# A window-attention and Fourier kernel: the order of ScalarE, VectorE and GpSimd written by hand as well as TensorE's, with attention times values ahead of the scores and the softmax in three parts

## The chip, the cores and the metric

One core of a Trainium2 chip. The metric is the device time of one execution in microseconds; the median of some runs is quoted. In the lines of the profile PE is TensorE's matmuls, PEld its weight loads, DVE is VectorE, ACT ScalarE, POOL GpSimd and SP SyncE; L12 is line 12 of that kernel, `out<-in` names what an instruction writes and reads, and brackets hold the engine's idle time before it and what ended it.

## The reference, cut to what matters

Two pre-normed residual layers on an image batch of 32 x 56 x 56 x 128, all fp32:

```python
x = x + swin_attention(group_norm(x))     # shifted 7x7 windows, 4 heads, rel. bias + mask, softmax, projection
x = x + fourier_block(group_norm(x))      # DCT along w and h, 32 modes mixed, inverse DCT, then
                                          # relu(h @ W1 + b1) @ W2 + b2, hidden width 512
```

## The kernel before

The kernel walks over 256 "rows": one row is the eight windows of one band of seven image lines, eight rows make an image. In each row, attention of one image runs next to a slice of the Fourier layer of the image before it. Row r computes q, k, v and the scores; two rows later the softmax is transposed, multiplied by the values and projected. The slices of the Fourier layer differ: I number the rows of an image c0 to c7 after them. c0 to c2 transform, c3 to c5 mix the modes, c4 to c7 transform back; all but c3 hold a group of the feed-forward (320 tokens in c4, 256 in c5, 512 elsewhere). At the ends of c2, c3 and c4 groups of the next image are transposed, and c5 does its norm.

TensorE's order is that of the source; the other engines are ordered by a scheduler:

```python
with tc.manual_schedule(engines={mybir.EngineType.PE}):
    ...
    for cycle in range(...):
        full_first(cycle)      # transposes of row-2, q, k of this row, zT transposes, feed-forward in
        ...
        half_columns(cycle)    # v of this row; DCT or mode mixing
        quarters(cycle)        # scores of this row, inverse DCT, values of row-2
        full_last(cycle, norm) # norm, feed-forward out, projection of row-2, groups of the next image
```

The parts that the argument touches (cut):

```python
def attn_qk(im, i):                       # ScalarE and VectorE empty k in turns
    for h in range(NH):
        if h % 2: nc.vector.tensor_scalar(dst, pk3[hs], im.bias[hs, 1:2], None, ALU.add)
        else:     nc.scalar.activation(dst, pk3[hs], AF.Identity, bias=im.bias[hs, 1:2])

def attn_scores(im, i, r):
    ...                                   # 64 matmuls
    for hp in range(2): nc.vector.tensor_tensor(a3, ps[hp], bm, ALU.add)
    nc.vector.tensor_reduce(mx2, a3, axis=AX.X, op=ALU.max)
    nc.gpsimd.tensor_tensor(a3, a3, mx2..., ALU.subtract)
    nc.scalar.activation(a3, a3, AF.Exp)
    nc.vector.tensor_reduce(sm2, a3, axis=AX.X, op=ALU.add)
    nc.vector.reciprocal(rs2, sm2)
    nc.gpsimd.tensor_tensor(a3, a3, rs2..., ALU.mult)

def image_norm(im):                       # small operations of the next image's norm
    nc.tensor.matmul(pg, lhsT=gavg, rhs=mv[:, 0:1], ...)
    nc.vector.tensor_copy(gm, pg[:, 0:1])
    nc.vector.tensor_tensor(d, mv[:, 0:1], gm, ALU.subtract)
    nc.vector.scalar_tensor_tensor(out=e, in0=d, scalar=d, in1=mv[:, 1:2], op0=ALU.mult, op1=ALU.add)
    yield
    nc.tensor.matmul(pv, lhsT=gavg, rhs=e, ...)      # the "second norm matmul"
    ...
```

PSUM, the memory that TensorE writes, is used as two rings of four banks: pa for attention, pc for the Fourier layer. Other names in the lines: oT is attention times values, xw a transposed group of the next image, hid the hidden layer of the feed-forward, zT the transposed modes that the inverse transform starts from, xf its result. A matmul group can start only when the bank that was taken four allocations earlier has been emptied.

## Time and profile before

| | kernel before |
|---|---|
| median time, us | 4475.1 (3 runs, 4466.23 to 4480.21) |
| TensorE busy, share of the span | 91% |
| mean granted clock | 0.963 |
| TensorE idle per image, us (mean of 27 or 28 images) | 10.1 |
| time at half clock per image, us | 7.9 |

The last two rows are read from the trace: between the first q matmul of one row and of the next, idle time is what no matmul record covers, and the clock records say how long the clock was at half. An image takes 135.1 us.

### The profile page before, as it was taken

The numbers are of one execution on the slowest core, as the hardware profiler recorded it, in microseconds if no ns is written. First come the engines' busy times: TensorE is split into PE (matmuls) and PEld (weight loads), VectorE is DVE, ScalarE is ACT, GpSimd is POOL, SyncE is SP. The second block draws the span as 40 slices with busy tenths as digits, with TensorE's granted clock in tenths as the row PEclk, the third lists the DMA queues.
The fourth block names the chain that finished last, engine by engine and source line by source line (L and its number), as shares of the span: only waits on it lengthen the run. The fifth ranks groups of instructions, "written<-read, shape, count | busy, mean of one in ns | idle before, by whom it ended". The sixth has DMA issues, their size and how long they took to land.

```text
span 4472.3 us, 165690 instructions
## 1 busy us (share of the span) xinstructions
PE 4051.8 (91%) x74816; PEld 3326.9 (74%) x74816; DVE 2485.8 (56%) x5078; ACT 2258.0 (50%) x4065; POOL 1386.7 (31%) x1358
## 2 busy tenths in 40 slices
PE   4789999899999999999999999999999999999999
PEld 3667777777777777777777777777777777777777
DVE  3655565555555555555555655555555555555551
ACT  1345555455555555555555555555545555555544
POOL 2323332233323333332333332333322333333321
PEclk8789999999999999999999999999999999999999
DMA  3111222212222212222212222212222212222112
GB/s 85 47 33 53 68 69 67 63 43 61 66 68 69 59 45 63 69 69 67 61 44 64 69 69 67 56 46 68 69 67 69 55 46 68 63 72 64 46 51 66
DMA packets 533831, 273.07 MB, mean 61 GB/s; under 512 B 29796, under 2 KB 532741, under 8 KB 532869
## 3 DMA queue, kind: packets, MB, share of 16 engines
q1 hardware_dynamic: 522072, 257.04, 21.9%
q8 instruction: 587, 9.62, 0.9%
q10 hardware_dynamic: 11052, 5.44, 0.5%
q14 instruction: 120, 0.97, 0.1%
HBM read 159.60 MB, written 102.76 MB: 59 GB/s over the span
## 4 chain that ended last, share of the span: by engine, by line
PE 70%; DVE 15%; POOL 6%; ACT 3%; issue 3%; DMA 2%; ACTq 1%; SPq 0%; POOLq 0%; DVEq 0%
PE pc L645 15%; PE pc L665 9%; PE pa L340 6%; PE pa L320 6%; PE pc L560 5%; PE pa L380 5%; PE pc L523 5%; POOL a L362 4%; PE pa L304 4%; DVE a L353 4%; PE pa L299 4%; DVE mx L361 4%; PE pa L436 4%; DVE sm L366 3%; ACT a L365 3%
## 5 line engine op out<-in xcount | busy, mean ns | idle before, releaser
L665 PE MATMUL pc<-wff,hid 128*128 128x128 f32 (+1 forms) x6400 | 786.5, 280 | 44.7 <-DVE xf L613 23.7
L665 PEld LDWEIGHTS pc<-wff,hid 128*128 128x128 f32 (+1 forms) x6400 | 737.8, 191 | 69.4 <-DVE xf L613 30.4
L362 POOL TENSOR_TENSOR a<-a,mx 128x784 f32<-128x784 f32 x256 | 388.5, 1518 | 1182.8 <-DVE mx L361 1170.0
L353 DVE TENSOR_TENSOR a<-pa,bm 128x392 f32<-128x392 f32 x512 | 266.3, 562 | 859.4 <-PE pa L340 859.4
L645 PE MATMUL pc<-xf,wff 128*128 128x512 f32 (+2 forms) x1792 | 710.4, 539 | 0.0
L653 ACT ACTIVATE hid<-pc,b1sb 128x512 f32<-128x512 f32 (+2 forms) x896 | 537.2, 632 | 77.8 <-PE pc L645 70.7
L365 ACT ACTIVATE a<-a 128x784 f32<-128x784 f32 x256 | 223.6, 873 | 677.4 <-POOL a L362 677.4
L368 POOL TENSOR_TENSOR a<-a,rs 128x784 f32<-128x784 f32 x256 | 389.0, 1519 | 545.7 <-DVE rs L367 519.9
L635 POOL TENSOR_TENSOR res<-res,b2sb 128x512 f32<-128x512 f32 (+2 forms) x256 | 263.7, 1035 | 905.1 <-DMA res<-scr 739.5
L645 PEld LDWEIGHTS pc<-xf,wff 128*128 128x128 f32 x1792 | 329.9, 190 | 275.1 <-issue 228.1
L366 DVE TENSOR_REDUCE sm<-a 128x16 f32<-128x784 f32 x256 | 248.2, 970 | 474.1 <-ACT a L365 474.1
L310 DVE TENSOR_SCALAR k_bd<-pa,bqkv 32x392 f32<-32x392 f32 x512 | 320.7, 626 | 269.3 <-ACT k_bd L312 261.3
L436 PE MATMUL pa<-wproj,oT 128*112 128x128 f32 x1792 | 266.5, 292 | 195.5 <-DVE oT L425 128.4
L436 PEld LDWEIGHTS pa<-wproj,oT 128*112 128x112 f32 x1792 | 226.9, 188 | 218.8 <-issue 167.2
L455 ACT ACTIVATE sq<-xl 112x384 f32<-112x384 f32 (+1 forms) x256 | 147.8, 578 | 440.0 <-DVE xl L444 333.9
L386 DVE COPY aT<-pa 128x512 f32<-128x512 f32 x512 | 336.7, 679 | 0.7 <-PE pa L380 0.7
L380 PE MATMUL pa<-ident,a 128*128 128x128 f32 x2048 | 314.7, 302 | 13.3 <-DVE xl L444 12.4
L340 PE MATMUL pa<-k_bd,q 64*64 64x49 f32 x16384 | 310.0, 221 | 17.3 <-ACT k_bd L312 8.6
L312 ACT ACTIVATE k_bd<-pa,bqkv 32x392 f32<-32x392 f32 x512 | 298.1, 582 | 54.7 <-PE pa L304 19.5
L320 PEld LDWEIGHTS pa<-wn,xw 128*64 128x64 f32 x4096 | 219.5, 137 | 133.9 <-issue 60.3
L252 POOL TENSOR_TENSOR xl<-xl,bproj 112x384 f32<-112x384 f32 (+1 forms) x256 | 285.0, 1141 | 80.9 <-PE pa L237 77.7
L340 PEld LDWEIGHTS pa<-k_bd,q 64*64 64x64 f32 x16384 | 273.0, 135 | 46.3 <-issue 15.8
(86 smaller groups left out, 6260.9 us busy)
## 6 DMA issues: line engine op xcount, KB each, us to landing
htok<-scr SPq DMA_DIRECT2D x256, 196.0 KB
res<-scr SPq DMA_DIRECT2D x160, 256.0 KB
out_dram<-res SPq DMA_DIRECT2D x128, 256.0 KB
scr<-xl SPq DMA_DIRECT2D x128, 224.0 KB
xl<-in_x_dram SPq DMA_DIRECT2D x32, 784.0 KB
xl<-in_x_dram SPq DMA_DIRECT2D x32, 672.0 KB
scr<-xl SPq DMA_DIRECT2D x128, 168.0 KB
out_dram<-res SPq DMA_DIRECT2D x96, 128.0 KB
```

Source lines behind the costliest of these rows:

```text
L320: nc.tensor.matmul(pv[w % 2 * JP : (w % 2 + 1) * JP, (w // 2) * C : (w // 2 + 1) * C], lhsT=im.xw[i][:, w * WT : w * WT + JP], rhs=im.w[:, ...
L340: nc.tensor.matmul(ps[hp][u * JP : (u + 1) * JP, w * WT : (w + 1) * WT], lhsT=q[cs, w * WT : w * WT + JP], rhs=k_bd[cs, w, u], start=True, ...
L353: nc.vector.tensor_tensor(a3, ps[hp][:, :RT].rearrange("p (m j) -> p m j", j=WT), bm[:, i // (NWR - 1), hp], ALU.add,)
L362: nc.gpsimd.tensor_tensor(a3, a3, mx2.unsqueeze(2).to_broadcast([P, 2 * NR, WT]), ALU.subtract)
L365: nc.scalar.activation(a3, a3, AF.Exp)
L366: nc.vector.tensor_reduce(sm2, a3, axis=AX.X, op=ALU.add)
L368: nc.gpsimd.tensor_tensor(a3, a3, rs2.unsqueeze(2).to_broadcast([P, 2 * NR, WT]), ALU.mult)
L380: nc.tensor.transpose(pt[:, m * P : (m + 1) * P], a[:, hp, 2 * pr : 2 * pr + 2].rearrange("p w j -> p (w j)"), ident,)
L436: nc.tensor.matmul(pp[:TC, (n - n0) * C : (n - n0 + 1) * C], lhsT=oT[:, (n - base) * TC : (n - base + 1) * TC], rhs=wproj, start=True, sto ...
L645: nc.tensor.matmul(ph[:, :n], lhsT=wff1[:, f * P : (f + 1) * P], rhs=xff[:, t0 : t0 + n], start=True, stop=True,)
L653: nc.scalar.activation(hf[:, :n], ph[:, :n], AF.Relu, bias=b1sb[:, f : f + 1])
L665: nc.tensor.matmul(pf[:m, c * C : (c + 1) * C], lhsT=im.hid[f][:, c * P : c * P + m], rhs=wff2[:, f], start=(f == 0), stop=(f == NF - 1),)
```

## The change

Its intent: take the remaining waits off TensorE by deciding the order on every engine. Values go before the scores, so that their result (oT) can be emptied while the scores run. The softmax becomes add, maximum and subtract after the scores, exp at the end of the row, sum and multiply in the next row. The norm and the statistics are cut into smaller steps. Groups of the next image go ahead of the projection.

```diff
-        nc.vector.reciprocal(rs2, sm2)
+    def attn_exp(r):
+        nc.scalar.activation(a3, a3, AF.Exp)
+    def attn_divide(r):
+        nc.vector.tensor_reduce(sm, a3, axis=AX.X, op=ALU.add)
+        nc.vector.reciprocal(rs, sm)
+        nc.gpsimd.tensor_tensor(a3, a3, rs..., ALU.mult)
 ... full_first
             for width, g in back_groups(c):
                 modes_transpose(im, width, g)
+        if row(cycle - 1)[0]:
+            attn_divide(cycle - 1)
+        next(norm)
         ...                                    # feed-forward in, statistics
+        next(norm)
 ... quarters, now small_tiles
+        attn_values(im, i, cycle - 2)
         attn_scores(im, i, cycle)
         ...                                    # modes_back
-        attn_values(im, i, cycle - 2)
 ... full_last
         ff_out(...)
+        attn_exp(cycle)
+        next(norm)
+        ...image_group(images[b + 1], j)
         attn_project(im, j)
-        ...image_group(images[b + 1], j)
-    with tc.manual_schedule(engines={mybir.EngineType.PE}):
+    with tc.manual_schedule(engines={ET.PE, ET.Activation, ET.DVE, ET.Pool}):
```

(The norm and the statistics gain `yield`s at other places, and the norm starts one row earlier.)

## The prediction

> **What bounds the kernel now.** I read the page first (busy time by engine, chain by engine), then cut the trace into windows, one for each row of attention, then TensorE's waits, and last the timeline of the rows with the longest waits.
>
> ```profile
> PE 4051.8 (91%) x74816; PEld 3326.9 (74%) x74816; DVE 2485.8 (56%) x5078; ACT 2258.0 (50%) x4065; POOL 1386.7 (31%) x1358
> ...
> PE 70%; DVE 15%; POOL 6%; ACT 3%; issue 3%; DMA 2%; ACTq 1%; SPq 0%; POOLq 0%; DVEq 0%
> ```
>
> TensorE is 91% busy and 70% of the chain; no other engine is near full. TensorE's program stays nearly the same, so the change can only win or lose the idle part, and the time at a lowered clock that idling brings. Eight rows make one image. Here is one image, a window per row (columns: length; busy us and instructions of PE, PEld, DVE, ACT, POOL; granted clock; DMA share; GB/s). I call the rows c0 to c7 in this order.
>
> ```profile
> 2212.25:2229.49 17.24, 17.03 (x320) 13.92 (x319) 9.81 (x22) 9.88 (x16) 3.65 (x5) 1.00 0.71 184
> 2229.49:2244.44 14.95, 14.95 (x263) 11.72 (x261) 8.04 (x17) 7.89 (x13) 4.12 (x5) 1.00 0.43 105
> 2244.44:2261.08 16.64, 15.85 (x269) 12.32 (x268) 9.96 (x20) 9.22 (x17) 5.69 (x6) 1.00 0.15 42
> 2261.08:2274.78 13.70, 11.68 (x306) 9.97 (x305) 8.09 (x17) 7.29 (x15) 6.66 (x8) 1.00 0.15 43
> 2274.78:2292.84 18.06, 16.80 (x343) 14.68 (x343) 11.24 (x24) 11.53 (x23) 7.28 (x8) 1.00 0.11 30
> 2292.84:2312.46 19.62, 16.79 (x319) 15.10 (x317) 10.81 (x28) 9.87 (x21) 6.94 (x7) 0.88 0.17 47
> 2312.46:2330.24 17.78, 16.63 (x275) 12.68 (x275) 9.32 (x19) 7.10 (x13) 4.42 (x4) 0.94 0.03 9
> 2330.24:2346.23 15.99, 15.23 (x261) 11.86 (x260) 9.95 (x21) 7.37 (x13) 4.41 (x4) 1.00 0.16 43
> ```
>
> Length minus PE busy is TensorE's idle time: 2.0 us in c3, 1.3 in c4, 2.8 in c5, under 1.2 elsewhere. Averaged over the 27 images between rows 30 and 250 the idle is 0.84, 0.45, 0.71, 2.09, 1.24, 3.11, 0.83, 0.79 us: 10.1 of 135.1 us. In c5 and c6 the clock falls too: 7.9 us per image run at half clock (averaged the same way), which costs up to 3.9. Both together, 14 us or 10%, are all that a better order could win. What TensorE waits for:
>
> ```profile
> PE pa L436 <- DVE oT L425: 128.4, 96, 4.3
> PE pa L436 <- DVE ve L274: 65.2, 31, 3.6
> ...
> PE pc L665 <- DVE xf L613: 23.7, 42, 0.8
> ```
>
> The output projection (L436) waits for the evacuation of attention times values (oT). Row c3 shows why:
>
> ```profile
> 2267.33 1.15 PE L340 MATMUL pa<-k_bd,q 64*64 64x49 f32 x64
> ...
> 2268.51 1.04 DVE L353 TENSOR_TENSOR a<-pa,bm 128x392 f32<-128x392 f32 x2 [2.87 <-PE pa L340]
> ...
> 2269.59 0.97 DVE L361 TENSOR_REDUCE mx<-a 128x16 f32<-128x784 f32 x1
> ...
> 2270.47 0.66 DVE L425 TENSOR_SCALAR oT<-pa,bqkv 128x147 f32<-128x147 f32 x3
> 2270.70 1.52 POOL L362 TENSOR_TENSOR a<-a,mx 128x784 f32<-128x784 f32 x1 [5.31 <-DVE mx L361]
> 2271.28 1.10 PE L436 MATMUL pa<-wproj,oT 128*112 128x128 f32 x8 [1.64 <-DVE oT L425]
> ...
> 2272.25 0.87 ACT L365 ACTIVATE a<-a 128x784 f32<-128x784 f32 x1 [2.07 <-POOL a L362]
> ...
> 2273.03 1.24 ACT L247 COPY xw<-pa 128x392 f32<-128x392 f32 x3
> ...
> 2273.63 1.06 PE L380 MATMUL pa<-ident,a 128*128 128x128 f32 x8
> ```
>
> Scores (L340) end at 2268.4; VectorE adds the mask and takes the maximum before it empties oT, so TensorE stands for 1.64 us. The last two lines matter later: exp, then the copies of the next image's groups (L247), end 5.8 us after the scores.
>
> **What the Trainium skill says.** "TensorE: Matmul & The Clock Gate", Part 1, table of states: half clock after an idle window of about 3.4 us, full clock after a busy one. The trace agrees on the two levels and on the free-running window, but less idleness is enough: of the 61 falls to half clock the median came after a window in which PE was 40% busy, and none above 68%; a gap of about 2 us does it. The same page, section "Architectural detail": ScalarE, VectorE and GpSimd queues are strictly first in, first out, so a hand-written order makes every wait hold up all that stands behind it. The busy trace of before fits this; it can't show an out-of-order start. "PSUM — Partial Sum Buffer", Terms: it is engines in the same bank and quadrant that collide. The four evacuations of k lie in different quadrants, yet this kernel makes them take turns: in the list of waits VectorE's k_bd waits 261.3 us in total for ScalarE's. That serial chain (ScalarE 0.58, VectorE 0.63, ScalarE 0.58, VectorE 0.63 us) stays.
>
> **The change part by part.** I worked rows by hand: program order of the built kernel, measured durations, four banks used in turn for attention (pa) and four for the rest (pc). T is the end of a row's scores, E the end of its projection.
>
> 1. *Values before scores, oT emptied at once.* Removes the L436 waits: 0.99 (c4) + 1.89 (c3) + 2.08 (c5) + 0.39 (c6) = 5.35 us per image.
> 2. *Norm and statistics spread.* Removes 0.79 us before the norm's last matmuls (L286) in c5. But the second norm matmul now waits inside c5 for VectorE's in-order list (k_bd, sum 0.97, reciprocal 0.25, three small operations 0.55): about 1.1 us, and the first for a bank, 0.55. Balance -0.9.
> 3. *Exp at the end of the row, ahead of the group copies on ScalarE.* In c3 no feed-forward matmuls follow the scores. Adds 1.04 + maximum 0.97 + subtract 1.52 + exp 0.88 + first group copy 0.48 + hops 0.3 = T+5.2 us. TensorE does 1.35 us of group transposes and 0.95 of projection, then the softmax transposes want the first group's bank: a wait of 2.9 us. After that k waits 0.8 us for the residual add, behind three statistics of 0.56 each on VectorE. The old order also reached these transposes 5.2 us after the scores (2273.63), but had 0.75 us of values in between.
> 4. *ScalarE in order: second k_bd copy ahead of zT and hid.* That copy waits for VectorE's k_bd, itself behind residual add, two sums, two aT copies: E + 0.65 + 1.2 + 1.3 + 0.63 = E+3.9; ScalarE's copy to E+4.5, zT to E+5.1. The third feed-forward matmul group needs zT's bank; TensorE gets there at E+4.8 with 512 columns (waits 0.3 and 0.4 in c7 and c6), and much earlier in c4 and c5, with groups of 320 and 256 columns and a late residual add: 1.7 and 1.3 us. The old order slipped zT and hid in ahead of the second copy.
> 5. *Values no longer between the scores and the inverse transform.* In c6 and c7 the second feed-forward product waits for the first xf add, T + 1.04 + 0.97 + 0.56 + hops = T+2.7. TensorE is there at T+1.66 or T+1.35, not 0.75 later as before: waits of 1.05 and 1.4 instead of 0.2 and 0.55, so +1.7 together.
> 6. *Rows with full feed-forward and no groups (c0, c1)* and c2: c0 keeps 0.6 for the statistics, c1 and c2 come out at 0. c3 has 0.9 at its v matmuls for aT. c6 and c7 have 0.2 and 0.1 for the copy of v.
>
> Sum of idle per image after: 0.6 + 0 + 0 + 0.9 + (2.9 + 0.8 + 1.7) + 2.95 + 1.65 + 1.8 = 13.3 us against 10.1, so +3.2. The stretch from 320 to 4317 us is 237 rows, 29.6 images: +95 us. Half clock: now certain at the c3/c4 border but partly hidden behind the 1.7 us wait, likely (three in four) in c5: 3.5 us lost per image, as much as before; 0. The first 18 rows (62 to 320 us, clock 0.80) have little TensorE work and are bound by the round through softmax; sharing it over three rows shortens a row of 12 to 15 us by about 1: -20 us. Total +75: 4550 us. Of the 10.1 us, some 1.5 stand in L398 groups with fewer than 64 records and are probably missing records, not idling; without them the old idle is 8.5 and the loss larger by up to 45. I put the prediction at 4555 us.
>
> **The rivals.** (a) The intended win: with the L436 waits gone TensorE never stands over 1 us, the clock stays full, and most of the 14 us go: 29.6 x 10 = about 300 us less, 4180. For it: the largest listed waits are just those removed, and VectorE and ScalarE are only half busy. Against it: points 3 to 5, each a wait on program order that half-busy engines don't cure. (b) ScalarE or VectorE becomes the bound: they have 11.5 us of work in the fullest row of 18, so no; only latency does. (c) The new idle pieces keep the clock at half for twice as long, 15 us per image: 4475 + 29.6 x 7 = 4680. (d) GpSimd's in-order residual load (L635 waits 739.5 us in all for its DMA) delays the subtraction. The data land about 6 us into the row and the subtraction is due after 12, so it is hidden; were it not, 1 us in seven rows would be 200 us.
>
> **Range and chances.** Each row estimate may be 0.3 us off, all in one direction at worst: 8 x 0.3 x 29.6 = 70 us; the clock adds some 50 either way. 8 in 10: 4440 to 4650. The 2% marks are 4386 and 4565: faster 0.10, same 0.44, slower 0.46.
>
> **What would show it.** Right: no wait of L441 (the projection's new line) on oT; waits of the softmax transposes (L385) on the group copies (L247) of nearly 3 us in c3; of the feed-forward's first product (L652) on zT (L594) in c4 and c5; of its second (L672) on xf (L620) above 1 us. Wrong: PE busy above 95%, a granted clock over 0.98 in the middle stretch, or transposes not held at c3, which would mean that the bank order was read wrongly or that the chain through exp is shorter than the old trace has it.

## The result, and the profile after

| | before | after |
|---|---|---|
| median time, us | 4472.5 (4 runs) | 4594.3 (4 runs, 4591.85 to 4597.65) |
| ratio | | 1.0272 (95%: 1.0253 to 1.0291) |
| TensorE busy, share of the span | 91% | 88% |
| TensorE idle per image, us | 10.1 | 14.0 |
| time at half clock per image, us | 7.9 | 9.3 |
| length of an image, us | 135.1 | 140.0 |

A ratio here is the mean time of one kernel's fast runs over that of the other's of the same rounds, so it is not quite the ratio of the medians. The change made the kernel 2.7% slower. The lengthening of an image, 4.8 us times the 29.6 images of the steady stretch, is 142 us; the first 18 rows ended 16 us earlier (row 18 starts at 304.0 us instead of 320.1). That sums to 126, and the two profiled runs lie 123.5 us apart.

One image of the changed kernel, cut as the prediction cuts the kernel before, c0 first (length; busy us of PE, PEld, DVE, ACT, POOL; granted clock; DMA share; GB/s):

```profile
2262.07:2280.40 18.33, 17.04 (x321) 13.92 (x320) 12.90 (x24) 9.29 (x17) 4.83 (x4) 1.00 0.70 175
2280.40:2296.03 15.63, 15.05 (x263) 11.99 (x262) 8.74 (x16) 7.82 (x13) 4.27 (x3) 1.00 0.42 99
2296.03:2311.66 15.63, 15.54 (x269) 12.48 (x268) 9.31 (x18) 8.84 (x16) 6.13 (x7) 1.00 0.18 52
2311.66:2326.51 14.85, 11.85 (x307) 10.39 (x306) 9.55 (x20) 7.06 (x14) 6.30 (x9) 0.97 0.12 32
2326.51:2346.70 20.19, 18.38 (x344) 14.96 (x344) 10.59 (x22) 11.36 (x22) 6.77 (x9) 0.94 0.08 22
2346.70:2368.10 21.40, 16.97 (x319) 15.07 (x318) 11.91 (x25) 9.64 (x20) 5.72 (x7) 0.84 0.10 29
2368.10:2385.39 17.29, 15.91 (x277) 12.07 (x276) 10.78 (x21) 7.79 (x13) 4.27 (x3) 1.00 0.11 31
2385.39:2402.88 17.49, 15.52 (x261) 11.67 (x260) 10.73 (x21) 7.51 (x13) 4.28 (x3) 1.00 0.15 42
```

Row c2 got shorter (16.5 us on average before, 15.6 after). The fourth line (c3) stands 3.0 us, the sixth (c5) 4.4 us, and c5 has only 0.84 of the clock. By waits (us in total, times, longest), TensorE's top four of the changed kernel:

```profile
PE pa L385 <- ACT xw L247: 100.4, 35, 3.2
PE pc L652 <- ACT zT L594: 98.5, 119, 3.4
PE pa L273 <- DVE e L268: 85.4, 32, 5.9
PE pc L672 <- DVE xf L620: 54.0, 51, 1.5
```

None of these four was above 24 us before. The two waits of the projection that led the old list (128.4 and 65.2 us) are gone; 1.9 us are left of the first. So the intended gain came, and new waits took more than it gave. Row c3 in the timeline of the changed kernel shows the first of them:

```profile
2318.83 1.15 PE L341 MATMUL pa<-k_bd,q 64*64 64x49 f32 x64
...
2321.09 0.97 DVE L358 TENSOR_REDUCE mx<-a 128x16 f32<-128x784 f32 x1
2321.18 1.06 PE L441 MATMUL pa<-wproj,oT 128*112 128x128 f32 x8
2322.20 1.51 POOL L359 TENSOR_TENSOR a<-a,mx 128x784 f32<-128x784 f32 x1 [2.71 <-DVE mx L358]
...
2323.75 0.87 ACT L365 ACTIVATE a<-a 128x784 f32<-128x784 f32 x1 [4.39 <-POOL a L359]
2324.53 1.24 ACT L247 COPY xw<-pa 128x392 f32<-128x392 f32 x3
...
2325.14 1.56 PE L385 MATMUL pa<-ident,a 128*128 128x128 f32 x8 [2.90 <-ACT xw L247]
```

The projection starts with no wait now. But the transposes behind it need a bank that holds a group of the next image; its copy (L247) stands behind exp on ScalarE, and exp stands behind maximum and subtract. ScalarE idles for 4.39 us, most of it with a copy in its list that could run. The transposes then take 1.56 us instead of 1.06: the clock records put a fall to half at 2325.55.

Row c5 shows something that the prediction had not foreseen:

```profile
2352.98 1.52 POOL L373 TENSOR_TENSOR a<-a,rs 128x784 f32<-128x784 f32 x1 [4.83 <-DVE rs L372]
2353.06 1.45 DVE L266 TENSOR_TENSOR d<-mv,gm 128x1 f32<-128x1 f32 x1
2354.45 0.72 POOL L642 TENSOR_TENSOR res<-res,b2sb 128x256 f32<-128x256 f32 x1
2354.54 0.65 DVE L268 SCALAR_TENSOR_TENSOR e<-d,mv 128x1 f32<-128x1 f32 x1
2355.24 0.59 PE L273 MATMUL pa<-e,gavg 128*128 128x1 f32 x2 [2.56 <-DVE e L268]
```

Two VectorE operations on one element per partition took 1.45 and 0.65 us. Here are their groups (busy us, mean ns), first in the changed kernel, then in the kernel before, where they are short on average:

```profile
L266 DVE TENSOR_TENSOR d<-mv,gm 128x1 f32<-128x1 f32 x32 | 45.1, 1409 | 1.1
L268 DVE SCALAR_TENSOR_TENSOR e<-d,mv 128x1 f32<-128x1 f32 x32 | 19.4, 606 | 1.1
```

```profile
L267 DVE SCALAR_TENSOR_TENSOR e<-d,mv 128x1 f32<-128x1 f32 x32 | 7.0, 220 | 1.1
L265 DVE TENSOR_TENSOR d<-mv,gm 128x1 f32<-128x1 f32 x32 | 6.4, 199 | 1.1
```

Each long one ended just as a GpSimd instruction ended: the first at 2354.51 with L373 (2354.50), the second at 2355.19 with L642 (2355.17). Both have two tensor inputs in SBUF. The Trainium skill, "GPSIMD Engine Reference", section 1 (Specifications), says that GpSimd shares its SBUF interfaces with VectorE and contends with VectorE instructions "with two SBUF inputs". The trace fits, with 1.41 us on average instead of 0.20 for the first and 0.61 instead of 0.22 for the second. In all images each long one ended within 0.02 us of a GpSimd instruction.

The old trace had this too, under its means. There d met GpSimd's addition to the residual in 6 of 32 images and was long once:

```profile
1085.74 1.29 DVE L265 TENSOR_TENSOR d<-mv,gm 128x1 f32<-128x1 f32 x1
```

GpSimd's L635 ran from 1085.74 to 1087.02. The operation nm of the Fourier layer's statistics, which has two SBUF inputs as well, took 0.16 us alone there and up to 1.10 beside L635, 0.35 on average; in the changed kernel it takes 1.41 in row c0, where no wait of TensorE hangs on it.

### The profile page after: what moved, and what is told of

Read it like the earlier page. It is cut to its first block, busy times and chain, and to the rows that moved or that the text cites. A ratio compares the mean times of both kernels' runs of the same rounds, so it can differ in the third digit from the quotient of the medians.

```text
span 4595.8 us, 165485 instructions
## 1 busy us (share of the span) xinstructions
PE 4058.6 (88%) x74816; PEld 3302.7 (72%) x74816; DVE 2707.2 (59%) x5078; ACT 2224.6 (48%) x4065; POOL 1368.6 (30%) x1358
## 5 line engine op out<-in xcount | busy, mean ns | idle before, releaser
L373 POOL TENSOR_TENSOR a<-a,rs 128x784 f32<-128x784 f32 x256 | 389.3, 1521 | 1939.8 <-DVE rs L372 1708.7
L652 PE MATMUL pc<-xf,wff 128*128 128x512 f32 (+2 forms) x1792 | 746.9, 549 | 98.5 <-ACT zT L594 98.5
L652 PEld LDWEIGHTS pc<-xf,wff 128*128 128x128 f32 x1792 | 320.3, 190 | 416.4 <-issue 194.1
L430 DVE TENSOR_SCALAR oT<-pa,bqkv 128x147 f32<-128x147 f32 (+2 forms) x768 | 171.8, 280 | 649.4 <-PE pa L403 649.1
L660 ACT ACTIVATE hid<-pc,b1sb 128x512 f32<-128x512 f32 (+2 forms) x896 | 501.1, 635 | 43.5 <-PE pc L652 37.5
L681 DVE TENSOR_TENSOR res<-pc,res 128x512 f32<-128x512 f32 (+2 forms) x256 | 144.1, 573 | 570.5 <-PE pc L672 396.1
L385 PE MATMUL pa<-ident,a 128*128 128x128 f32 x2048 | 280.8, 282 | 101.4 <-ACT xw L247 100.4
L321 PEld LDWEIGHTS pa<-wn,xw 128*64 128x64 f32 x4096 | 243.6, 148 | 145.9 <-issue 61.0
L350 DVE TENSOR_TENSOR a<-pa,bm 128x392 f32<-128x392 f32 x512 | 266.2, 562 | 128.4 <-PE pa L341 128.2
L391 DVE COPY aT<-pa 128x512 f32<-128x512 f32 x512 | 325.4, 677 | 0.4 <-PE pa L385 0.4
L321 PE MATMUL pa<-wn,xw 128*64 128x128 f32 x4096 | 311.3, 299 | 12.5 <-ACT q L301 9.6
L385 PEld LDWEIGHTS pa<-ident,a 128*128 128x128 f32 x2048 | 240.3, 146 | 108.1 <-issue 100.0
```

What stands on the lines that cost most here:

```text
L321: nc.tensor.matmul(pv[w % 2 * JP : (w % 2 + 1) * JP, (w // 2) * C : (w // 2 + 1) * C], lhsT=im.xw[i][:, w * WT : w * WT + JP], rhs=im.w[:, ...
L373: nc.gpsimd.tensor_tensor(a3, a3, rs.unsqueeze(2).to_broadcast([P, 2 * NWR, WT]), ALU.mult)
L385: nc.tensor.transpose(pt[:, m * P : (m + 1) * P], a[:, hp, 2 * pr : 2 * pr + 2].rearrange("p w j -> p (w j)"), ident,)
L391: nc.vector.tensor_copy(aT.rearrange("p m a j -> p (m a j)"), pt)
L652: nc.tensor.matmul(ph[:, :n], lhsT=wff1[:, f * P : (f + 1) * P], rhs=xff[:, t0 : t0 + n], start=True, stop=True,)
L660: nc.scalar.activation(hf[:, :n], ph[:, :n], AF.Relu, bias=b1sb[:, f : f + 1])
```

## The experiments

Theory A: the loss is a sum of separate waits, each made by one place in the hand-written order of ScalarE, VectorE or GpSimd. Rival C: the waits are one chain, and a wait that is taken away comes back at the next place. A further rival, put to the test in the second half, blames TensorE's new order. In all kernels but the seventh TensorE's order is exactly that of the changed kernel (compared instruction by instruction; in the traces 10 to 90 of the 74816 matmuls change places with another that starts at nearly the same time). All results were correct, and every timed run had three rounds.

| run | median us | ratio to before (95%) | idle per image | half clock per image |
|---|---|---|---|---|
| changed kernel | 4594.3 | 1.0272 (1.0253 to 1.0291) | 14.0 | 9.3 |
| 1 exp after groups | 4513.9 | 1.0105 (1.0079 to 1.0131) | 12.7 | 7.2 |
| 2 zT before k | 4531.6 | 1.0141 (1.0116 to 1.0166) | 12.7 | 10.0 |
| 3 norm before divide | 4472.0 | 1.0010 (0.9982 to 1.0037) | 11.7 | 4.1 |
| 4 xf before maximum | 4566.6 | 1.0220 (1.0194 to 1.0245) | 13.2 | 8.8 |
| 5 all four | 4200.3 | 0.9396 (0.9377 to 0.9415) | 5.8 | 0.3 |
| 6 TensorE's order alone | 4277.2 | 0.9570 (0.9555 to 0.9584) | 7.8 | 0.5 |
| 7 hand order alone | 5363.5 | 1.1998 (1.1969 to 1.2027) | 29.4 | 31.6 |
| 8 norm with one input | 4532.8 | 1.0140 (1.0123 to 1.0157) | 13.0 | 5.2 |
| 9 all four, norm earlier | 4165.4 | 0.9322 (0.9301 to 0.9343) | 4.7 | 0.8 |

The kernel before had medians of 4467.7 (beside runs 1 to 4), 4469.0 (5 to 8) and 4467.0 (9). The gains told below are differences of medians of different rounds. By the ratios, each good to some 10 us, the first four are 75, 59, 117 and 23 us instead of 80, 63, 122 and 28, and that of run 5 is 392 instead of 394.

**1. Exp after the group copies.**

```diff
-        if row(cycle)[0]:
-            attn_exp(cycle)
         next(norm)
         ...image_group(images[b + 1], j)
+        if row(cycle)[0]:
+            attn_exp(cycle)
         attn_project(im, j)
```

> The changed kernel with one move: ScalarE's exp stands after the copies of the next image's groups instead of before them (TensorE's order is the same). Theory A (each wait on program order costs what the trace shows): the wait of the softmax transposes on the group copies in the fourth row of each image, 2.9 us, goes; about 0.7 us of it comes back as k waiting for the residual add. 29.6 images x 2.2 = 65 us less than the changed kernel, so about 4530 us (ratio to before 1.013). Theory C (the waits are one chain, a removed one comes back at the next place): within 15 us of 4594.

Measured: 80 us less than the changed kernel; in the traces the steady images give 66 of it, as expected, and the first 18 rows 16. The wait at the transposes went wholly (2.89 us per image to 0). In c4 the wait on zT grew from 0.72 to 2.00 and k waits 0.3 us for the residual add, so part of the gain came back, though less of it than Theory C says; time at half clock fell by 2.1 us. From the longest waits of this run:

```profile
PE pc L652 <- ACT zT L594: 135.9, 119, 3.4
```

It was 98.5 us in the changed kernel: TensorE now reaches that place earlier and finds the same late copy.

**2. zT ahead of the last two evacuations of k.**

```diff
         for h in range(NH):                  # in attn_qk: now only h = 0, 1
 ...
                 modes_transpose(im, width, g)
+        attn_k(im, 2, NH)                    # h = 2, 3
         if row(cycle - 1)[0]:
             attn_divide(cycle - 1)
```

> The changed kernel with one move: the third and fourth evacuation of k (ScalarE, then VectorE) stand after the zT copies instead of before them (TensorE's order is the same). Theory A: the waits of the feed-forward's first product on zT (0.72 + 1.60 + 0.52 + 0.37 = 3.2 us per image by the trace) go: 29.6 x 3.2 = 95 us less, about 4500 us (ratio 1.006), and a little more where the clock falls less. Theory C: within 15 us of 4594, with the third k_bd evacuation and the scores waiting instead.

Measured: 63 us less, short of the 95. The waits on zT went in all four rows (3.2 us per image to 0). The miss is one line of the waits of this run:

```profile
PE pa L273 <- DVE e L268: 140.4, 32, 5.9
```

85.4 us before, 4.4 instead of 2.5 us per image: in c5 TensorE came to the second norm matmul 1.9 us sooner (4.15 us after the row's start instead of 6.06), and e was no earlier (8.51 in both). That wait had been hidden behind the other.

**3. Norm ahead of divide.**

```diff
+        next(norm)
         if row(cycle - 1)[0]:
             attn_divide(cycle - 1)
-        next(norm)
```

> The changed kernel with one move: the small norm operations on VectorE (gm, d, e) stand before the softmax's sum and reciprocal, so that GpSimd's multiply is not yet running when they are (TensorE's order is the same). Theory A with contention: d and e, which took 1.41 and 0.61 us while GpSimd was at work, fall back to the 0.20 and 0.22 us of the kernel before; the wait of the second norm matmul (2.5 us per image) goes wholly, and the half clock in that row (6.3 us per image) becomes rarer: 29.6 x 2.5 = 75 us, and 20 to 60 more from the clock, so 4460 to 4520 us. If list order alone matters and not contention, d stays near 1.4 us and only about 1.2 of the 2.5 us go (4560).

Measured: 122 us less, the largest of the four and inside the expected interval, with a swap of two lines. d and e took 0.16 and 0.22 us, no wait of that matmul is left in the steady rows, and half clock in c5 fell from 6.3 to 0.6 us per image. Row c5 went from 22.0 to 17.4 us: 2.5 us of wait, and about 2 more because TensorE no longer runs c5 at half clock. The swap alone doesn't separate contention from list order; run 8 does.

**4. xf ahead of the maximum.**

```diff
                 modes_back(im, width, g)
+                if todo:                     # after the first group
+                    attn_max(cycle)          # maximum and subtract, taken out of attn_scores
+                    todo = False
```

> The changed kernel with one move: in rows with an inverse transform the first two xf additions stand on VectorE before the softmax maximum instead of after it (TensorE's order is the same). Theory A: the wait of the feed-forward's second product on xf in the seventh and eighth row falls from 1.0 and 1.4 to about 0.1 and 0.4 us: 29.6 x 1.9 = 55 us less, 4540 us (ratio 1.015). Theory C: the later softmax comes back as a wait on exp or the sums, within 15 us of 4594.

Measured: 28 us less, half of what was expected. In c7 the wait fell from 1.20 to 0.36 us, as foretold; in c6 from 0.63 to 0.06, where I had used 1.0 as its size. In c6 another 0.35 us stands inside the matmul group just before (L609), for which the profile shows no wait; it did not go in this run (0.40), so it is not counted here. The rows themselves got shorter by 0.54 and 0.79 us, 39 us in all; 0.1 to 0.2 us per row came back in c4 and c5.

**5. All four moves.**

> The four moves of the runs before (exp after the group copies, zT before the third k evacuation, norm before divide, xf before the maximum) in one kernel. Theory A (separate waits): the gains add, 80 + 63 + 122 + 28 = 293 us, and what two of them gave back (zT waits 1.3 us per image longer in the first, norm wait 1.9 us longer in the second) is saved as well, 40 to 90 us: 4210 to 4300 us, ratio to before 0.945 to 0.963, faster than both kernels. Theory C (one chain): no better than the best single move, about 4470.

Measured: 394 us less than the changed kernel and 6.0% less than before. The four single gains sum to 293. The other 101 fit the table: idle time fell by 2.5 us per image more than in the four runs together (74 us), mostly what runs 1 and 2 had lost to the next wait, and time at half clock by 1.9 us more (28 us), since the clock stays up here (half clock 0.3 us per image). Theory C falls. It was right in one thing: two of the waits stood one behind the other, so that a single gain understates the worth of the set.

**6. TensorE's new order, the other engines left to the scheduler.**

```diff
-    with tc.manual_schedule(engines={ET.PE, ET.Activation, ET.DVE, ET.Pool}):
+    with tc.manual_schedule(engines={ET.PE}):
```

> The changed kernel's source, but with only TensorE's order written by hand, as in the kernel before; ScalarE, VectorE and GpSimd are ordered by the scheduler. Theory A: values ahead of the scores frees oT (5.4 us per image of waits go, as in the changed kernel), and the scheduler places zT and the norm early as it did before; a wait on the group copies and on xf stays: 4380 to 4470 us, ratio 0.98 to 1.0. Rival (the loss lies in TensorE's new order, not in the hand order of the others): 4560 to 4600.

Measured: 4277, better than I expected and 4.3% faster than before. So the change is two parts of opposite sign: TensorE's new order with the finer source is worth 195 us (4472 to 4277), and the hand-written order of the other three costs 317 (4277 to 4594). The rival that blames TensorE's order falls. The scheduler's order has no wait on the group copies. The longest of TensorE's waits in this run:

```profile
PE pc L672 <- DVE xf L620: 56.1, 50, 1.5
```

This one, 1.9 us per image in c6 and c7, is as long as in the changed kernel (54.0): it comes with values ahead of the scores, under the scheduler's order of VectorE and under the first one by hand. It is not bound to TensorE's order: with xf ahead of the maximum, run 5 has 13.6 us left of it. With the four moves the order by hand is also better than the scheduler's, by 77 us (4200 against 4277).

**7. The kernel before, its own source order forced on all four engines.**

```diff
-    with tc.manual_schedule(engines={mybir.EngineType.PE}):
+    with tc.manual_schedule(engines={PE, Activation, DVE, Pool}):   # names shortened here
```

> The kernel before, whose source is left as it is but whose ScalarE, VectorE and GpSimd take the order of the source too. Theory A: VectorE then stands through subtract and exp (2.6 us) before it empties oT, in every row: waits of the projection of 1 to 6 us in each, 13 us and more per image above before, and more time at half clock: 4850 to 5050 us (ratio 1.09 to 1.13). Rival (the scheduler's order was no better than the source's): within 2% of before.

Measured: 5363, 20% slower and worse than the 13% that I gave. The direction is as expected. The first wait stands in c0 to c3 (1.6 to 5.6 us); the waits on xf in c4 to c7 I had not counted:

```profile
PE pa L436 <- DVE oT L425: 390.7, 128, 6.1
PE pc L665 <- DVE xf L613: 243.9, 60, 4.6
```

xf too stands behind the whole softmax in the source, and half clock rose to 31.6 us per image. A source written for a scheduler was no order to run as it stands. That splitting the softmax, as the change does, is what mends this was not tested on its own.

**8. d and e with one tensor input each, place and order unchanged.**

```diff
-        nc.vector.tensor_tensor(d, mv[:, 0:1], gm, ALU.subtract)
+        nc.vector.tensor_scalar(d, mv[:, 0:1], gm, None, ALU.subtract)
-        nc.vector.scalar_tensor_tensor(out=e, in0=d, scalar=d, in1=mv[:, 1:2], op0=ALU.mult, op1=ALU.add)
+        nc.vector.tensor_scalar(e, d, d, mv[:, 1:2], ALU.mult, ALU.add)
```

> The changed kernel with d and e of the norm computed in the same place and order, but each with one tensor input (the second operand given as a per-partition scalar). If the two operations were long because VectorE's second tensor input had to wait for GpSimd, they take about 0.16 us each though GpSimd's multiply still runs at that time; the wait of the second norm matmul falls from 2.5 to about 1.0 us: 29.6 x 1.5 = 45 us less, with the clock 30 to 80: 4515 to 4565 us. If any VectorE operation was slowed there by something else, they stay long: 4594.

Measured: 62 us less than the changed kernel. From the timeline of c5 in this run:

```profile
2049.17 1.52 POOL L371 TENSOR_TENSOR a<-a,rs 128x784 f32<-128x784 f32 x1 [4.83 <-DVE rs L370]
2049.25 0.21 DVE L266 TENSOR_SCALAR d<-mv,gm 128x1 f32<-128x1 f32 x1
2049.50 0.27 DVE L268 TENSOR_SCALAR e<-d,mv 128x1 f32<-128x1 f32 x1
...
2049.83 0.38 PE L271 MATMUL pa<-e,gavg 128*128 128x1 f32 x2 [0.95 <-DVE e L268]
```

GpSimd's multiply runs from 2049.17 to 2050.69, and both operations pass under it, each in about a quarter of a microsecond. The second tensor input is what had waited. The two-input form alone is not slow: in run 3, away from GpSimd, it took 0.16 and 0.22 us. The wait of the matmul is 0.9 us per image: that is the part due to plain list order, 1.6 us were contention.

**9. All four moves, and the norm ahead of the last two evacuations of k.**

```diff
+        next(norm)
         attn_k(im, 2, NH)
-        next(norm)
         if row(cycle - 1)[0]:
             attn_divide(cycle - 1)
```

> The kernel with all four moves, and the norm's small VectorE operations now ahead of the last two evacuations of k as well, in the time in which VectorE waits for ScalarE's evacuation. Theory A: the wait of the second norm matmul, 1.43 us per image in the run with four moves, goes to under 0.2: 29.6 x 1.3 = 38 us less than 4200, so about 4162 us, ratio to before 0.931. If it comes back as a wait of the scores on k, it stays at 4200.

Measured: 4165.4. The norm's matmul waits 0.15 us per image instead of 1.43. This is the fastest version found, 6.8% faster than before and 9.3% below the changed kernel (4165 against 4594), with the same instructions on TensorE in the same order as the changed kernel.

## Why the prediction was right or wrong

The time, 4594, lies in the range, 39 us above the 4555 predicted, and on the side (slower by over 2%) that had 0.46. Point by point, with the prediction's numbering; measured values are means per image:

1. *The projection's waits.* Right: 5.35 us were to go; no wait on oT is left in the steady rows (1.9 us in the whole run).
2. *The norm spread.* Right in kind, wrong in size, and the term of the sum that failed: "three small operations 0.55" and a wait of about 1.1 us. The wait was 2.5 us, because d and e took 1.41 and 0.61 us beside GpSimd, which I had not looked for: every estimate took a mean duration from the old trace. That trace already had d at 1.29 us once and nm at up to 1.10, both ending with GpSimd's instruction; e met only GpSimd's memset there, and kept its 0.22. Run 8 shows that one-input forms bring the wait to 0.9. The bank wait of 0.55 that I put before the first norm matmul did not occur.
3. *Exp ahead of the group copies.* Right: 2.9 us predicted at the transposes, 2.89 measured; run 1 removes it. The 0.8 us at k behind it did not show (0.05), and TensorE ran the matmuls ahead of it at the lowered clock (1.56 us for the transposes, which take 1.04 in c6 of the changed kernel at full clock), so it came later; that this hid the wait is argued, not tested.
4. *zT behind k.* Right in its place, half the size in c4: 1.7, 1.3, 0.4, 0.3 predicted for c4, c5, c6, c7; 0.72, 1.60, 0.52, 0.37 measured. (The sum for the second copy gives E+3.8, not 3.9, which changes nothing.) In c4 TensorE came late, after the wait of step 3 and at the lowered clock; in run 1, without that wait, it stood 2.00 us there. Run 2 removes all four.
5. *xf behind the maximum.* Right in c7, 1.4 (1.20 measured), and too long in c6, 1.05 (0.63). Run 6 shows the same wait with TensorE's new order alone, as the step says; runs 4 and 5 show that VectorE's order can take it away.
6. *The other rows.* c0 0.6 (0.86 measured, and on a bank that hid had to free, not on the statistics), c1 and c2 0. The 0.9 us of c3's v matmuls did not occur (0.09).

The sum of idle time was predicted as 13.3 us against a measured 14.0, and that is nearer than the working was. Of the 14.0, waits with a named cause are 11.7, and 2.3 are gaps inside or before matmul groups for which the profile shows no wait; before, these were 7.9 and 2.2. So the list of waits was 1.6 too long, misses of both signs cancel in it, and the gaps, which it did not hold, fill the rest. The prediction took 1.5 us of these gaps for missing records. No record is missing: both traces have all 74816 matmuls, with 64 in each group of values. What the gaps are stays open. The clock term failed more clearly: 3.5 us lost per image were foretold, "three in four" for c5; half clock came to 9.3 us, so about 4.6 lost, 6.3 of the 9.3 in c5 alone and in nearly every image. That is again the longer wait of step 2. The prediction's "a gap of about 2 us does it" holds often, not always: in the old trace 16 of the 26 projection waits between 1.8 and 2.1 us were followed by a fall within the next 3.5 us, and 17 of the 18 longer ones. The start-up gain, 20 us, was 16. Of the 39 us, 0.7 us more of idle is 21 and 0.7 us more of lost clock another 21, the start 4; less the 5 us that the prediction put on top of its 4550, and the 3 by which the kernel before was faster beside the changed one.

Of the rivals, (a), the intended win, describes run 6 and runs 5 and 9 better than it describes the change: the 4180 given for it is nearly what the order reaches once the new waits are gone. (c) did not come, but its direction was right. (b) and (d) did not: VectorE is 59% busy, and no run shows the subtraction waiting for the residual's data.

## What to carry to other kernels

When a scheduler's order is replaced by a list, the waits that it was dodging can come due: for every instruction that waits for another engine (exp, the second k evacuation), ask what stands behind it in the list that was ready, and whose bank that holds. Mend such waits together, since one hides behind another and the long ones cost the TensorE clock as well (29 of the 34 waits of 2.9 us on the group copies were followed by a fall): four small moves gave 80, 63, 122 and 28 us alone and 394 together. And take care with mean durations from the old trace: d lasted seven times as long where it met a neighbour that it had seldom met before. The longest of a group, looked up beside the mean, would have shown it.

## What the Trainium skill lacked or had wrong

- On the contention of VectorE with GpSimd nothing is lacking. "GPSIMD Engine Reference", section 1, gives neither its size nor the way round it, but the skill has both, on another page, "SBUF — State Buffer", in "Who interferes with whom". The numbers: a VectorE operation on 128x1 elements rose from 0.20 to 1.41 us on average, ending with GpSimd's instruction to 0.02 us; with a per-partition scalar in place of the second tensor input it took 0.21 us under the same GpSimd multiply.
- "TensorE: Matmul & The Clock Gate", the table of states in Part 1 and the closing table, speak of an idle window or of gaps above about 3 us. (A passage of Part 1 on queue cycling allows for frequent shorter idling, without a figure.) Shorter waits suffice here: in the changed kernel the clock fell 68 times, at the median after a 3.4 us window that was 32% busy, and up to 53%; in c5 a wait of 1.59 and one of 2.56 us, with 1.1 us of work between them, did it in every steady image.
